# Where the gate weights are loaded and summed, and where the first blocks' tiles lie, in a two-layer graph network kernel

## The chip, the cores and the metric

The kernel runs on one core of a Trainium2 chip. A core has a matrix engine (TensorE, PE in the profile; its weight loads are shown apart as PEld), VectorE (DVE), ScalarE (ACT), GpSimd (POOL) and SyncE (SP), which here only issues transfers. Each engine works through its own instructions in order and waits on semaphores for the others. Transfers (DMAs) are issued by SP and by ScalarE, and 16 DMA engines carry them out.

The metric is the device time of one execution in microseconds, the median of three runs.

## The reference, cut to what matters

There are two layers over 128 graphs of 128 nodes with 256 features, all in float32. Only the first layer is touched by the change:

```python
h = jnp.maximum(_layernorm(x, axis=-1), 0.0)
# _L0_gnn_ref(h, ...):
xc = jnp.transpose(h, (0, 2, 1))
t = relu(bn(conv1d(xc, conv1_w, 0)))                 # 1x1 convolution
t = bn(conv1d(t, conv2_w, 8))                        # 17 taps along the nodes
x_conv = jnp.transpose(relu(t + xc), (0, 2, 1))
s = h @ w_se.T + b_se                                # 3 features
A = jnp.exp(-dist(s)) * adj
x_nmp = A @ relu(h @ w_msg.T + b_msg)
gi = concatenate([x_conv, x_nmp], -1) @ w_ih.T + b_ih
gh = h @ w_hh.T + b_hh                               # gates r, z, n from gi and gh
x = x + (1 - z) * n + z * h
```

The second layer applies five small graph convolutions to the first 25 nodes of each graph, with a softmax of `fusion_w` as their weights.

## The kernel before, in words

A block is 4 graphs (`BB`), so there are 32 blocks. A half is 64 graphs, 16 blocks. The 17-tap convolution is done in the frequency domain: 40 frequencies (`NP_`), for which the transformed inputs of one half are kept on chip in one tile `X` (80 KB per partition).

**Heads of the first half** (`heads` with h = 0). For each block: load x (`head_load`, tile `ln`), statistics (`head_stats`: VectorE, then one power on POOL, tile `rs`, L193), normalise (`head_norm`, VectorE, L199), transpose and relu (`head_turn`, L209 and L210), the first convolution (`head_conv1`, L223 to L227), the transform into `X` (`head_spectra`, L238 to L246). Between these steps the transform of the 17-tap weights runs (`weight_spectra`) and is written to DRAM as `vd`.

**Frequencies of the first half** (`spectral` with h = 0). Two frequencies at a time, 1 MB of `vd` is loaded by SP into a tile `v` (three buffers, two DMAs each, L291). For each frequency POOL adds two parts of `v` into `vs` (L306), VectorE combines two parts of `X` into `s` (L304), and TensorE runs two groups of matmuls, L309 on `vs` and L314 on `s` and `X`. ScalarE and VectorE bring the result into `ys` (L311, L315). After every four frequencies ScalarE issues two writes of `ys` to DRAM (`yd`). A table `amid` lets other work be issued ahead of a frequency: the first blocks of the second half are begun there (`heads_begin`), and so are the loads of `idm`, `wms`, `bms` and `fw` (`small_loads`, at frequency 8), of `wih` (at 12) and of `whh` (at 20).

**Heads of the second half** (`heads` with h = 1). The same as before, with three x blocks ahead. The function `between` that `heads` calls twice per block here steps the generator `gate_weights` (L333 to L337). It forms sums and differences of blocks of the gate weights on POOL, since `gates` multiplies 2 by 2 blocks with seven products instead of eight. There are twelve such adds of 128 x 384 elements, two per step.

**Frequencies of the second half** (`spectral` with h = 1, nothing amid).

**Blocks** (from L421). `load(i)` brings a block's inputs from DRAM: `ht` (three buffers), the adjacency `at`, and the frequency results `ym` and `yr` (two buffers each). For each block: `messages` (L505), `conv_out` (L487 on `ym`, L490 on `yr`), `edge_terms`, `edges`, `x_nmp` (L551), then `gates` (L599). The second layer's work runs between the gate products. `load(0)` and `load(1)` stand ahead of the first block, followed by the loads for the node degrees (`degree_loads`).

**What sets the order.** The first stage is issued in the order written. In the stages of the halves that holds for POOL throughout and for SP up to the end of the second half's heads (`manual_schedule`); elsewhere a scheduler may move an instruction ahead. The block phase's pool `wk` reuses the memory of the front stages. `reuse_waits="tile"` means that a new tile waits until the last use of each old tile that lay there. Tiles are laid out in the order in which `load` first asks for them. DMAs take eight completion semaphores in turn, so that a DMA waits for the landing of the eighth one before it.

Of the kernel before, what the change touches and what calls it, by code (L numbers as in the profile page):

```python
# [8 lines left out]
F32 = mybir.dt.float32  # L9
# [4 lines left out]
P = 128  # L14
# [3 lines left out]
BB = 4  # L18
# [3 lines left out]
NP_ = LW // 2  # L22
# [52 lines left out]
def gnn_kernel(ctx: ExitStack, tc: tile.TileContext, io, out0: bass.AP, out1: bass.AP):  # L75
    nc = tc.nc
    x, adjT = io["x"], io["adjT"]
    B, N, D = x.shape
    C = D // P
# [15 lines left out]
    def row(name, n):  # L95

        return bass.AP(tensor=io[name].tensor, offset=io[name].offset, ap=[[0, P], [1, n]])
# [16 lines left out]
    def constant_loads():  # L114
        nc.sync.dma_start(vec, io["vec"])
        nc.sync.dma_start(wc1, io["wc1"].rearrange("(c p) o -> p c o", p=P))
        nc.sync.dma_start(fd, io["fd"])
# [23 lines left out]
    fw = cst.tile([P, 5], F32)  # L141
# [35 lines left out]
    def head_load(pool, ahead, i, queue):  # L177
        xs[i] = pool.tile([P, BB, D], F32, tag="ln", name="ln", bufs=ahead)
        queue.dma_start(xs[i], x[i * BB:(i + 1) * BB].rearrange("b n d -> n b d"))

    def head_stats(wk, i, behind=None):

        mv = wk.tile([P, BB, 2], F32, tag="mv", name="mv", bufs=3)
        st = wk.tile([P, BB, 6], F32, tag="st", name="st", bufs=2)
        if behind is not None:
            nc.scalar.copy(st[:, :, 0], behind[:, :, 0])
        for b in range(BB):
            nc.vector.bn_stats(st[:, b, :], xs[i][:, b, :])
            nc.vector.bn_aggr(mv[:, b, :], st[:, b, :])
        ve = wk.tile([P, BB], F32, tag="ve", name="ve", bufs=2)  # L190
        nc.vector.tensor_scalar(ve, mv[:, :, 1], EPS, None, op0=ALU.add)  # L191
        rs = wk.tile([P, BB], F32, tag="rs", name="rs", bufs=3)
        nc.gpsimd.tensor_tensor(rs, ve, mhalf, op=ALU.pow)  # L193
        stats[i] = mv, rs
# [19 lines left out]
    def head_conv1(wk, i):  # L214
        ht = hcs.pop(i)
        h1 = wk.tile([P, BB, D], F32, tag="h1", name="h1", bufs=2)
        for h in range(BB // 2):
            ps = bank()
            pv = ps.rearrange("p (b d) -> p b d", b=2)
            for bb in range(2):  # L220
                b = 2 * h + bb
                for c in range(C):
                    nc.tensor.matmul(pv[:, bb, :], ht[:, c, b * N:(b + 1) * N], wc1[:, c, :],  # L223
                                     start=c == 0, stop=c == C - 1)
            hv = h1[:, 2 * h:2 * h + 2, :]
            nc.vector.tensor_tensor(hv, pv, sh1[:, None, :].to_broadcast([P, 2, D]), op=ALU.add)
            nc.scalar.activation(hv, hv, AF.Relu)  # L227
        h1s[i] = h1
# [32 lines left out]
    def heads(wk, xk, ahead, X, h, between):  # L261

        i0, i1 = h * NBH, (h + 1) * NBH
        for i in range(i0, i1 + 1):
            if i + ahead < i1:
                head_load(xk, ahead, i + ahead, nc.sync)
            if i < i1:
                head_conv1(wk, i)
            between()
            if i + 1 < i1:  # L270
                head_turn(wk, i + 1)
            if i + 2 < i1:
                head_norm(i + 2)
            between()
            if i > i0:
                head_spectra(X, i - 1)
            if h == 0 and i % 2:
                between()
            if i + 3 < i1:
                head_stats(wk, i + 3, h1s[i] if h else None)  # L280
# [59 lines left out]
    with front as es:  # L340
        hk = es.enter_context(tc.tile_pool(name="hk", bufs=1))
        xp = es.enter_context(tc.tile_pool(name="xp", bufs=1))
        X = xp.tile([P, C, NP_, 2, P], F32)
        order = es.enter_context(ExitStack())
        order.enter_context(tc.manual_schedule(engines={nc.gpsimd.engine}))
        sync_order = order.enter_context(ExitStack())
        sync_order.enter_context(tc.manual_schedule(engines={nc.sync.engine}))
        with ExitStack() as ws:

            ws.enter_context(tc.manual_schedule())  # L350

            xk = ws.enter_context(tc.tile_pool(name="xk", bufs=1, side="right"))
            wp = ws.enter_context(tc.tile_pool(name="wp", bufs=1))
            ahead = 5
            todo = [(c, q) for c in range(C) for q in range(D // WCH)]
            head_load(xk, ahead, 0, nc.scalar)
            nc.sync.dma_start(gt, io["gt"])
            taps = [taps_load(wp, *todo[0], nc.sync, split=4)]
            spectra = []

            def some_spectra(k=1):
                for _ in range(k):
                    if not spectra and todo:
                        spectra.append(weight_spectra(wp, *todo.pop(0), taps.pop(0)))
                    if spectra and next(spectra[0], STOP) is STOP:
                        spectra.pop(0)
                        if len(todo) > 1:
                            taps.append(taps_load(wp, *todo[1], nc.scalar))
                        some_spectra()

            constant_loads()
            head_load(xk, ahead, 1, nc.sync)
            taps.append(taps_load(wp, *todo[1], nc.sync))
            for k in range(2, ahead):
                head_load(xk, ahead, k, nc.sync)
            head_stats(hk, 0)
            some_spectra()
            head_norm(0)
            some_spectra()
            head_turn(hk, 0)  # L380
            constants()
            some_spectra()
            head_stats(hk, 1)
            some_spectra()
            head_norm(1)
            head_stats(hk, 2)
            some_spectra()
            heads(hk, xk, ahead, X, 0, some_spectra)
            while spectra or todo:
                some_spectra()  # L390
        gw = ctx.enter_context(tc.tile_pool(name="gw", bufs=1, side="right", reuse_waits="tile"))
        xk = es.enter_context(tc.tile_pool(name="xk1", bufs=1, reuse_waits="tile"))
        bp = es.enter_context(tc.tile_pool(name="bp", bufs=1, reuse_waits="tile"))
        idm = gw.tile([P, N], F32)
        wms = gw.tile([P, C, D + 3], F32)
        bms = gw.tile([P, D + 3], F32)
        wih = gw.tile([P, 2 * C, 3 * D], F32)
        whh = gw.tile([P, C, 3 * D], F32)
        sw = [gw.tile([P, 3, 3, P], F32, name=f"sw{k}") for k in range(3)]

        def small_loads():
            nc.sync.dma_start(idm, io["idm"])
            nc.sync.dma_start(wms, io["wms"].rearrange("(c p) o -> p c o", p=P))
            nc.sync.dma_start(bms, row("bms", D + 3))
            nc.sync.dma_start(fw, row("fw", 5))

        begin = heads_begin(hk, xk, 3, 1)
        sums = gate_weights()
        amid = {p: lambda: next(begin, None) for p in range(16, NP_, 4) if p != 20}
        amid[8] = small_loads  # L410
        amid[12] = lambda: nc.sync.dma_start(wih, io["wih"].rearrange("(c p) o -> p c o", p=P))
        amid[20] = lambda: nc.sync.dma_start(whh, io["whh"].rearrange("(c p) o -> p c o", p=P))
        spectral(bp, X, 0, amid)
        for _ in begin:
            pass
        heads(hk, xk, 3, X, 1, lambda: next(sums, None))
        sync_order.close()
        spectral(bp, X, 1, {})
        order.close()

    wk = ctx.enter_context(tc.tile_pool(name="wk", bufs=1, reuse_waits="tile"))  # L421
# [4 lines left out]

    def load(i):
        h, g0 = divmod(i * BB, HG)
        ht = wk.tile([P, C, T], F32, tag="ht", name="ht", bufs=3)
        nc.sync.dma_start(ht, htd[i])  # L430
        at = wk.tile([P, BB, N], F32, tag="at", name="at", bufs=2)
        nc.sync.dma_start(at, adjT[i * BB:(i + 1) * BB].rearrange("b m n -> m b n"))
        y = yd[h].rearrange("g w d o -> g (w d) o")[g0:g0 + BB]
        ym = wk.tile([P, BB, D], F32, tag="ym", name="ym", bufs=2)
        nc.sync.dma_start(ym, y[:, :P, :].rearrange("g r o -> r g o"))
        yr = wk.tile([P, D], F32, tag="yr", name="yr", bufs=2)
        for b in range(BB):
            nc.sync.dma_start(yr[b * NR:(b + 1) * NR, :], y[b, P:, :])
        loaded[i] = at, ym, yr
        hts[i] = ht  # L440
# [698 lines left out]
```

## Time and profile before

| what | value |
|---|---|
| median of 3 runs | 1935.14 us (1934.36 to 1942.66) |
| the profiled execution | 1944.77 us, span 1943.0 us |
| mean granted TensorE clock | 0.992 |
| instructions | 29921 |
| bytes moved by DMA | 265.76 MB, mean 137 GB/s |

The stages, from the timeline: the heads of the first half end near 175 us, its frequencies near 292, the heads of the second half near 402, its frequencies near 507, and the blocks fill the rest. The page's chain of work that ended last begins with this line:

```profile
PE 90%; DMA 6%; DVE 2%; issue 1%; ACT 1%; POOL 0%; SPq 0%; ACTq 0%; POOLq 0%; DVEq 0%
```

The chain is followed back from the last instruction, at each step to what released it. Nine tenths of it is TensorE itself. The rows of DMAs on the page that belong to the stages in question are these, with how often each is issued and how large one is:

```profile
v<-vd SPq DMA_DIRECT2D x80, 512.0 KB
yd<-ys ACTq DMA_DIRECT2D x40, 512.0 KB
```

So each half's frequencies read 20 MB of `vd` and write 10 MB of `yd`.

### The profile page before, as it was taken

How to read it: one execution, taken by the hardware profiler on the slowest of the kernel's cores; microseconds unless marked ns; L12 is line 12 of the kernel's file. 1: busy time of each engine (PE TensorE's matmuls, PEld its weight loads, DVE VectorE, ACT ScalarE, POOL GpSimd, SP SyncE). 2: the span in 40 equal slices, each digit the busy share in tenths (PEclk: the TensorE clock that was granted, in tenths of full speed). 3: DMA queues.
4: the chain of work that ended last, by engine and by line, in shares of the span. 5: the costliest groups of instructions: out<-in, count | busy, mean ns of one | idle time of the engine just before them, and what ended most of it. 6: DMA issues, size and time to landing. Idle time of an engine off the chain costs nothing.

```text
span 1943.0 us, 29921 instructions
## 1 busy us (share of the span) xinstructions
PE 1901.1 (98%) x10418; PEld 1652.7 (85%) x10418; DVE 1296.3 (67%) x3247; ACT 713.2 (37%) x1459; POOL 609.2 (31%) x681
## 2 busy tenths in 40 slices
PE   8999898999899999999999999999999999999999
PEld 7888787988788888888888888888878888888887
DVE  5676457754587777777756577787756587777643
ACT  4553113421143334334333434334334434333334
POOL 1012442135233433443322243343322143343300
PEclk9999999999899999999999999999999999999999
DMA  8787975459843223233323533224333523222125
GB/s 309 293 315 226 323 260 194 142 181 309 267 135 98 72 72 102 68 81 110 81 84 92 142 81 100 70 71 116 86 82 87 147 75 105 74 72 64 44 88 154
DMA packets 248853, 265.76 MB, mean 137 GB/s; under 512 B 106850, under 2 KB 223927, under 8 KB 244223
## 3 DMA queue, kind: packets, MB, share of 16 engines
q1 hardware_dynamic: 236767, 196.74, 35.8%
q10 hardware_dynamic: 11936, 67.11, 8.9%
q8 instruction: 83, 1.36, 0.3%
q14 instruction: 67, 0.55, 0.1%
HBM read 178.66 MB, written 85.14 MB: 136 GB/s over the span
## 4 chain that ended last, share of the span: by engine, by line
PE 90%; DMA 6%; DVE 2%; issue 1%; ACT 1%; POOL 0%; SPq 0%; ACTq 0%; POOLq 0%; DVEq 0%
PE bank L599 44%; PE bank L314 6%; PE bank L505 5%; PE bank L919 5%; PE bank L859 5%; PE bank L223 5%; PE bank L487 3%; PE bank L551 3%; PE bank L238 3%; DMA v<-vd 3%; PE bank L309 3%; PE bank L490 1%; PE bank L162 1%; PE bank L538 1%; PE bank L838 1%; PE bank L770 1%
## 5 line engine op out<-in xcount | busy, mean ns | idle before, releaser
L599 PE MATMUL bank<-t,sw 128*128 128x256 f32 x1152 | 290.9, 379 | 0.2 <-POOL t L573 0.2
L612 POOL TENSOR_TENSOR u<-u,m 128x256 f32<-128x256 f32 x128 | 92.9, 726 | 594.4 <-ACT m L610 532.2
L599 PEld LDWEIGHTS bank<-t,sw 128*128 128x128 f32 x1152 | 215.3, 190 | 30.1 <-issue 2.3
L599 PE MATMUL bank<-t,wih 128*128 128x256 f32 x768 | 197.2, 379 | 0.0
L599 PEld LDWEIGHTS bank<-t,wih 128*128 128x128 f32 x768 | 143.4, 190 | 19.3 <-DVE u L617 0.5
L306 POOL TENSOR_TENSOR vs<-v 128x512 f32<-128x512 f32 x78 | 100.5, 1307 | 138.7 <-DMA v<-vd 74.9
L223 PE MATMUL bank<-wc,ht 128*128 128x256 f32 x512 | 125.1, 399 | 6.1 <-ACT ht L210 6.1
L505 PE MATMUL bank<-wms,ht 128*128 128x259 f32 x512 | 122.3, 381 | 0.0
L223 PEld LDWEIGHTS bank<-wc,ht 128*128 128x128 f32 x512 | 100.4, 201 | 22.6 <-ACT ht L210 8.4
L599 PE MATMUL bank<-t,whh 128*128 128x256 f32 x384 | 114.6, 380 | 0.3 <-DVE z L614 0.3
L599 PE MATMUL bank<-xc,wih 128*128 128x256 f32 x384 | 114.7, 380 | 0.0
L599 PE MATMUL bank<-xn,wih 128*128 128x256 f32 x384 | 114.6, 380 | 0.0
L919 PE MATMUL bank<-w,hh 128*125 128x256 f32 (+9 forms) x480 | 113.5, 380 | 0.3 <-DVE hh L864 0.3
L599 PE MATMUL bank<-ht,whh 128*128 128x256 f32 x384 | 110.3, 381 | 0.0
L505 PEld LDWEIGHTS bank<-wms,ht 128*128 128x128 f32 x512 | 97.3, 190 | 14.7
L304 DVE SCALAR_TENSOR_TENSOR s<-X 128x256 f32<-128x256 f32 x78 | 48.0, 618 | 90.4 <-PE bank L314 90.1
L859 PE MATMUL bank<-ax,w 128*128 128x500 f32 (+8 forms) x416 | 107.0, 396 | 0.0
L617 DVE TENSOR_TENSOR u<-bank,u 128x256 f32<-128x256 f32 x128 | 53.7, 420 | 74.0 <-PE bank L599 74.0
L919 PEld LDWEIGHTS bank<-w,hh 128*125 128x125 f32 (+9 forms) x480 | 84.3, 177 | 18.6 <-issue 0.9
L509 ACT ACTIVATE msg<-msg 128x512 f32<-128x512 f32 x64 | 40.3, 630 | 162.0 <-DVE msg L506 160.2
L193 POOL TENSOR_TENSOR rs<-ve,mhalf 128x4 f32<-128x4 f32 x32 | 32.3, 1010 | 211.7 <-DVE ve L191 211.7
L311 ACT COPY k<-bank 128x256 f32<-128x256 f32 x78 | 29.0, 373 | 179.4 <-PE bank L309 70.2
(191 smaller groups left out, 4305.3 us busy)
## 6 DMA issues: line engine op xcount, KB each, us to landing
v<-vd SPq DMA_DIRECT2D x80, 512.0 KB
vd<-sp ACTq DMA_DIRECT2D x8, 2560.0 KB
yd<-ys ACTq DMA_DIRECT2D x40, 512.0 KB
w<-in_w_dram SPq DMA_DIRECT2D x40, 512.0 KB
htd<-ht ACTq DMA_DIRECT2D x32, 512.0 KB
ht<-htd SPq DMA_DIRECT2D x32, 512.0 KB
ym<-yd SPq DMA_DIRECT2D x32, 512.0 KB
xt<-in_xT_dram SPq DMA_DIRECT2D x32, 512.0 KB
```

The source lines that it names most:

```text
L223: nc.tensor.matmul(pv[:, bb, :], ht[:, c, b * N:(b + 1) * N], wc1[:, c, :], start=c == 0, stop=c == C - 1)
L238: nc.tensor.matmul(ps[:, bb * 2 * LW:(bb + 1) * 2 * LW], h1[:, 2 * h + bb, c * P:(c + 1) * P], fd, start=True, stop=True)
L306: nc.gpsimd.tensor_tensor(vs, vr, vi, op=ALU.add)
L309: nc.tensor.matmul(p1[:, :D], a[:, c], vs[:, c], start=c == 0, stop=c == C - 1)
L314: nc.tensor.matmul(ps[:, k * D:(k + 1) * D], u[:, c], w[:, c], start=c == 0, stop=c == C - 1)
L487: nc.tensor.matmul(ps[:, b * N:(b + 1) * N], ym[:, b, o * P:(o + 1) * P], idm, start=b == 0, stop=False)
L505: nc.tensor.matmul(ps[:, :D + 3], ht[:, c, b * N:(b + 1) * N], wms[:, c, :], start=c == 0, stop=c == C - 1)
L551: nc.tensor.matmul(ps[:, b * N:(b + 1) * N], msg[:, b, c * P:(c + 1) * P], e[:, b, :], start=True, stop=True)
L599: nc.tensor.matmul(ps, w, d, start=n == 0, stop=n == len(pairs) - 1)
L612: nc.gpsimd.tensor_tensor(got["u4"], got["u2"], got["m5"], op=ALU.add)
L859: nc.tensor.matmul(pv[:, q - q0, :], w1s[k5 + g][:, c, q * P:(q + 1) * P], xv[:, c], start=c == 0, stop=c == C - 1)
L919: nc.tensor.matmul(ps[:n1, :D], hh[:, q, at:at + n1], w2s[k5 + g][:, q, :], start=q == 0, stop=q == HID // P - 1)
```

## The change

It has three parts.

- The load of `fw` (five numbers, for the second layer's softmax) moves from `small_loads` to the start, behind the first five x blocks. The few VectorE and ScalarE instructions that use it are moved by the scheduler from around the second half's frequencies to the first heads.
- The other weight loads move from the first half's frequencies to the heads of the second half. A new generator `gate_loads` takes the place of `gate_weights` as what `heads` steps between its parts; `wih` is loaded in two DMAs. The sums of `gate_weights` move to the frequencies of the second half, one step ahead of every fourth frequency from 4 on.
- `load` asks for its tiles in another order: `at`, `yr` and `ym` come before `ht`. With that `yr` of block 0 no longer lies on `X`, and `ht` of block 1 does. The order of the DMAs stays.

The order of TensorE's instructions is the same in both programs. POOL's adds L333 to L337 stand among L306 instead of L193.

```diff
             for k in range(2, ahead):
                 head_load(xk, ahead, k, nc.sync)
+            nc.sync.dma_start(fw, row("fw", 5))
...
             nc.sync.dma_start(bms, row("bms", D + 3))
-            nc.sync.dma_start(fw, row("fw", 5))
...
         amid = {p: lambda: next(begin, None) for p in range(16, NP_, 4) if p != 20}
-        amid[8] = small_loads
-        amid[12] = lambda: nc.sync.dma_start(wih, io["wih"].rearrange("(c p) o -> p c o", p=P))
-        amid[20] = lambda: nc.sync.dma_start(whh, io["whh"].rearrange("(c p) o -> p c o", p=P))
         spectral(bp, X, 0, amid)
         for _ in begin:
             pass
-        heads(hk, xk, 3, X, 1, lambda: next(sums, None))
+
+        def gate_loads():
+            yield
+            small_loads()
+            yield
+            yield
+            nc.sync.dma_start(wih[:, :C], io["wih"][:D].rearrange("(c p) o -> p c o", p=P))
+            yield
+            yield
+            nc.sync.dma_start(wih[:, C:], io["wih"][D:].rearrange("(c p) o -> p c o", p=P))
+            yield
+            yield
+            nc.sync.dma_start(whh, io["whh"].rearrange("(c p) o -> p c o", p=P))
+
+        loads = gate_loads()
+        heads(hk, xk, 3, X, 1, lambda: next(loads, None))
         sync_order.close()
-        spectral(bp, X, 1, {})
+        spectral(bp, X, 1, {p: lambda: next(sums, None) for p in range(4, NP_, 4)})
+        for _ in sums:
+            pass
...
     def load(i):
         h, g0 = divmod(i * BB, HG)
+        at = wk.tile([P, BB, N], F32, tag="at", name="at", bufs=2)
+        yr = wk.tile([P, D], F32, tag="yr", name="yr", bufs=2)
+        ym = wk.tile([P, BB, D], F32, tag="ym", name="ym", bufs=2)
         ht = wk.tile([P, C, T], F32, tag="ht", name="ht", bufs=3)
         nc.sync.dma_start(ht, htd[i])
-        at = wk.tile([P, BB, N], F32, tag="at", name="at", bufs=2)
         nc.sync.dma_start(at, adjT[i * BB:(i + 1) * BB].rearrange("b m n -> m b n"))
         y = yd[h].rearrange("g w d o -> g (w d) o")[g0:g0 + BB]
-        ym = wk.tile([P, BB, D], F32, tag="ym", name="ym", bufs=2)
         nc.sync.dma_start(ym, y[:, :P, :].rearrange("g r o -> r g o"))
-        yr = wk.tile([P, D], F32, tag="yr", name="yr", bufs=2)
```

## The prediction

> **What bounds the kernel now.** I read, in this order: the busy shares on the page, the list of what TensorE waited for, the busy table cut at the stages that the diff touches, and the timeline around each TensorE gap. TensorE is busy for nearly the whole span, so time can come only from its gaps and from its clock.
>
> ```profile
> PE 1901.1 (98%) x10418; PEld 1652.7 (85%) x10418; DVE 1296.3 (67%) x3247; ACT 713.2 (37%) x1459; POOL 609.2 (31%) x681
> PEclk9999999999899999999999999999999999999999
> ```
>
> 1943.0 - 1901.1 leaves 41.9 us of gaps. The mean granted clock of 0.992 costs another 1943 x 0.008 = 15 us. The list of waits says who ended the gaps:
>
> ```profile
> PE bank L162 <- DMA w<-in_w2t_dram: 7.8, 2, 5.7
> PE bank L223 <- ACT ht L210: 6.1, 6, 2.9
> PE bank L309 <- POOL vs L306: 5.9, 4, 3.0
> PE bank L314 <- issue: 4.5, 2, 2.5
> PE bank L490 <- DMA yr<-yd: 2.9, 1, 2.9
> ```
>
> Rows two to five lie in four stages: the frequencies of the first half, the heads of the second half, the frequencies of the second half, and the start of the block phase. Their busy table:
>
> ```profile
> 175.10:291.80 116.70, 106.26 (x482) 91.33 (x482) 54.95 (x98) 16.16 (x43) 53.20 (x43) 0.99 0.84 278
> 291.80:402.00 110.20, 104.68 (x620) 94.89 (x619) 82.89 (x260) 47.77 (x135) 24.84 (x24) 0.98 0.45 157
> 402.00:507.00 105.00, 105.00 (x494) 92.55 (x493) 49.71 (x83) 16.05 (x45) 47.13 (x39) 1.00 0.83 274
> 507.00:526.00 19.00, 14.07 (x61) 11.13 (x60) 9.67 (x22) 4.15 (x7) 6.08 (x8) 0.76 0.89 250
> ```
>
> The columns are length, then busy PE, PEld, DVE, ACT, POOL, then clock, DMA share, GB/s. The two halves do the same frequency work. The second half, without weight loads among its `v` loads, has no gap at all. The first half has 10.4 us of gaps. The places, from the timeline:
>
> ```profile
> 191.94 0.77 SPq L411 DMA_DIRECT2D wih<-in_wih_dram  x1
> 237.07 1.78 DVE L199 TENSOR_SCALAR ln<-ln,mv,rs 128x256 f32<-128x256 f32 x2 [5.14 <-POOL rs L193]
> 240.35 2.03 PE L314 MATMUL bank<-v,s 128*128 128x256 f32 x4 [1.99 <-issue]
> 301.26 4.31 DVE L199 TENSOR_SCALAR ln<-ln,mv,rs 128x256 f32<-128x256 f32 x4 [1.13 <-POOL rs L193]
> 307.37 0.70 PE L223 MATMUL bank<-wc,ht 128*128 128x256 f32 x2 [2.93 <-ACT ht L210]
> 330.77 1.38 DVE L199 TENSOR_SCALAR ln<-ln,mv,rs 128x256 f32<-128x256 f32 x4 [1.12 <-POOL rs L193]
> 507.12 1.98 SPq L438 DMA_DIRECT2D yr<-yd  x4
> 514.37 1.19 PE L490 MATMUL bank<-idr,yr 128*128 128x256 f32 x2 [2.94 <-DMA yr<-yd]
> 515.00:520.00 5.00, 5.00 (x16) 3.31 (x14) 2.17 (x3) 1.61 (x3) 0.72 (x1) 0.50 0.95 284
> ```
>
> The same four L199 take 4.31 us at 301 and 1.38 at 331: at 301 four gate sums run on POOL beside them, at 331 none do. The five microseconds after the `yr` gap run at clock 0.50.
>
> [...] after 2.98 us of idle at 194.8 no slow slice shows, so not every gap pays. [...]
>
> **The change part by part.** The instruction lists of both programs show the same order on TensorE. So each part is only a matter of what comes late.
>
> *Loads out of the first half's frequencies.* Removed there: idm, wms, bms, fw (455 KB), wih 1536 KB, whh 768 KB, together 2.8 MB, or 10 us at that stage's 278 GB/s. The gaps are 2.98 + 1.73 + 0.92 + 0.29 = 5.9 us before L309 (`v` late, hence `vs` late) and 1.99 + 2.53 = 4.5 us before L314. The latter come from VectorE: L199 stands in front of `s` (L304) and waits for `rs`, which sits on POOL behind the `vs` of a late tile. The slice 240 to 245 has clock 0.66, another 1.7 us. All of it: 12.1. The 5.9 should go, as in the second half. The order L199 before `s` stays: with the second half's timing `vs` of frequency 23 would end as TensorE starts L309 of 22, and rs 1.0 + two L199 0.75 + s 0.42 = 2.2 us set against the 0.86 us of that L309 still stalls about 1.4. For the three norms I keep 2 us. Gain 10 (5 to 12).
>
> *The same loads among the second half's heads.* DMA share is 0.45 there, 157 GB/s. 2.8 MB add 26 GB/s over 110 us. Each lies in SP's queue between x loads that are 6.5 us apart; 768 KB need 2.8 us. Only the first three meet the last `v` tiles, near 297 to 304, where the queue is full; the x block loaded then is read about 6 us later. Cost 0 (0 to 3).
>
> *Sums out of these heads.* Both L199 groups shrink from 4.31 to 1.38 us. The first sum burst ends in gaps of 2.93 and 0.31, the second in 0.93 and 0.31; ScalarE then offers `ht` at about 304.5 against TensorE's 304.4, so some 0.4 stays. The slices 305 to 315 have clocks 0.86 and 0.79: 0.7 + 1.05 = 1.75 us. Gain 4.1 + 1.4 = 5.5 (3 to 6.5). The fill gap of 1.06 at 297.6 stays.
>
> *Sums into the second half's frequencies.* Twelve adds of 1.0 us, in pairs of 2.15 before frequencies 4 to 24. POOL goes from 47 to 60 of 105 us. POOL idles between the `vs` of one tile and of the next: the six places have 1.46 us or more. At frequency 12 the idle is 1.60, so `vs` comes 0.55 later, and it now leads L309 by 434.36 - 431.83 = 2.5. At 20 the lead is only 0.26, but the idle before it is 3.63. [...] This cover is all that hides 12.9 us. Cost 0.5 (0 to 12).
>
> *Tiles laid out elsewhere.* In the program's layout `yr` of block 0 lay on the tile X, so its four loads waited at SP for the last L314 at 506.7, with everything of block 1 behind them. Now at, yr and ym of block 0 lie below X and block 1's `ht` reaches into it instead. The `yr` loads go out near 498 to 500 behind 1.4 MB (ht, at, ym, idr; about 5 us at 274 GB/s), landing by 505; L490 wants them at 511.4. Block 1's ht then waits for X in their place, issued near 507 instead of 512.3, and is read at 526.7. Gain 2.94, plus 1.6 of the 2.5 us that the 0.50 slice costs; the 1.99 us gap before L551, VectorE's `e`, remains [...]. Gain 4.5 (2.9 to 5.5).
>
> *fw load early.* Its six tiny VectorE instructions (about 0.16 us each, as L191 shows) and one ScalarE exponential move into the first heads. Between x loads it should land near 19 us (4.9 MB at about 330 GB/s); VectorE reads it at 23.5. Two come just ahead of the add L226 at 33.2. Cost 0.5 (0 to 1.5, more if fw lands late, because VectorE's whole queue waits behind the reduction).
>
> Sum: 10 + 5.5 + 4.5 - 0 - 0.5 - 0.5 = 19 us. The profiled execution took 1944.77, 9.6 above the median of 1935.14. The trace does not say where those 9.6 went. The 57 us of gaps and slow clock are the natural place, and the change removes a third of that, so I take a third of 9.6, about 3, as already absent from the median run: 1935 - 16 = 1919.
>
> **Rivals.**
> 1. The first half stays bound by its own `v` and `yd` traffic (DMA share 0.84) and by L199 before `s`; only 3 of the 10 come. For: after the weight loads were through, gaps still came at 231, 238 and 263. Against: the second half has the same traffic and none. Gain 12, less the 3: 1926.
> 2. The loads make the x blocks late among the heads, undoing that 5.5 and costing 2: gain about 11, less 2: 1926. Against: share 0.45.
> 3. The other side. The pairs of sums hold up `vs` in the second half. It begins to cost once pair 2.15 exceeds idle plus lead, 4.1 at frequency 12. Then TensorE stops up to 2.15 us six times (12.9), each stop followed by a slow slice of 1.7 (10), and `s` blocked for 0.9 us on a dozen frequencies (11). 34 us against 20 gained: 1947.
> 4. Everything goes, the norm stalls and the whole 0.50 slice too: 24 us, 1911 or less.
>
> **How the numbers follow.** Forecast 0.58 at 1919, own range 1911 to 1926; rival 1 0.17, rival 2 0.08, rival 3 0.09, rival 4 0.08. A difference of 0.5%, 9.7 us, is about what a measurement of this kernel tells from none: faster means below 1925.5. Faster: 0.54 of the forecast + 0.08 + 0.05 + 0.03 = 0.70; slower 0.09; the rest 0.21. The range 1909 to 1932 leaves out rival 3 and the far ends.
>
> **What would show it.** Right: the first half's frequencies take about 106 us from first L309 to last L314, with no wait on POOL `vs`; four L199 take about 1.4 us at every head; no wait of L490 on `yr`, no 0.50 slice; the second half still without gaps. Wrong: waits of L309 on `vs` in the second half, x loads landing after VectorE is ready, VectorE waiting for fw near 24 us, or the first half's gaps unchanged.

## The result, and the profile after

| | before | after |
|---|---|---|
| median, runs side by side | 1939.41 us (14 runs, 1932.32 to 1944.15) | 1929.74 us (14 runs, 1922.02 to 1935.02) |
| profiled execution | 1944.77 us, span 1943.0 | 1930.41 us, span 1928.7 |

The ratio is 0.995, with a 95% interval from 0.9936 to 0.9964: a gain of 9.7 us, between 7.0 and 12.4. The forecast was 19 us on the profiled execution and 16 on the median. The measured time lies above the forecast's own range of 1911 to 1926 us, though within the outer one of 1909 to 1932. Part of that is the base, whose median over 14 runs is 4.3 us higher than over the three runs of the prediction. The gain itself is 9.7 of the 16 us forecast for the median; the two profiled executions differ by 14.4, against 19.

The busy shares and the clock on the page of the changed kernel:

```profile
PE 1900.0 (99%) x10418; PEld 1654.8 (86%) x10418; DVE 1288.2 (67%) x3247; ACT 712.2 (37%) x1459; POOL 610.3 (32%) x681
PEclk9899999999999999999999999999999999999999
```

TensorE's gaps are 1928.7 - 1900.0 = 28.7 us instead of 41.9. Who ended them is in its list of waits (us in total, times, longest):

```profile
PE bank L162 <- DMA w<-in_w2t_dram: 7.7, 2, 5.8
PE bank L565 <- DVE e L555: 2.4, 2, 2.1
...
PE bank L309 <- POOL vs L306: 2.4, 1, 2.4
PE bank L723 <- DVE dinv L718: 2.3, 1, 2.3
...
PE bank L223 <- ACT ht L210: 1.6, 3, 1.1
...
PE bank L314 <- DVE s L304: 0.2, 1, 0.2
PE bank L314 <- issue: 0.2, 1, 0.2
```

Lines from L434 of the kernel before are 14 higher here: L490 is L504, L551 is L565, L709 is L723. The wait on `yr` is gone, L223 and L309 wait a good deal less. One line is larger than before, L723 on `dinv`, which had 0.8 us. It will matter.

The busy table at the same four stages (length, then busy PE, PEld, DVE, ACT, POOL, then clock, DMA share, GB/s):

```profile
178.40:285.80 107.40, 104.64 (x485) 90.60 (x484) 53.04 (x92) 15.99 (x42) 49.25 (x39) 1.00 0.84 273
285.80:392.70 106.90, 105.06 (x635) 95.79 (x634) 79.01 (x266) 48.60 (x139) 18.89 (x18) 1.00 0.55 191
392.70:495.20 102.50, 102.50 (x476) 90.06 (x475) 48.80 (x79) 15.00 (x40) 58.19 (x49) 1.00 0.85 282
495.20:507.80 12.60, 10.42 (x56) 8.60 (x56) 6.58 (x18) 4.04 (x7) 6.09 (x8) 0.91 0.83 222
```

As these lines stand, they seem to confirm the sum term by term: the first half's frequencies from 117 to 107 us, the second half's heads from 112 to 107, the second half's frequencies without a gap although 58 us of POOL lie there, the start of the blocks from 17.5 to 12.6. That is 20 us. (The values of before are taken between the marks below, which put the heads at 112.3 us; the prediction's table cuts them at rounder times.) A pair of profiles is not the median, however, and two stages lie outside this table: the first heads, and the first two blocks. The experiments had to tell where 20 us became 10.

**How stages are measured below.** From the traces, between marks that exist in every variant: the first heads end with the first L309, a half's frequencies end with the last L314 of that half, the second half's heads lie between, the start of the blocks ends with the first gate product (L599 before, L613 after), and "two blocks" are the gates of blocks 0 and 1 with all between them. Blocks 2 to 31 took 1292.43 or 1292.44 us in all seventeen traces, so nothing is to be found there. Half clock means a spell in which the trace records a granted TensorE clock of 0.50; what is lost to it is estimated as half the length of the spell (in the run with late transposes and the old layout sixteen L238 took 4.63 us in such a spell and 2.44 outside).

### The profile page after: what moved, and what is told of

The parts are those of the page before. It is cut to its first block, busy times and chain, and to the rows that moved or that the text cites. A ratio compares the mean times of both kernels' runs of the same rounds, so it can differ in the third digit from the quotient of the medians.

```text
span 1928.7 us, 29906 instructions
## 1 busy us (share of the span) xinstructions
PE 1900.0 (99%) x10418; PEld 1654.8 (86%) x10418; DVE 1288.2 (67%) x3247; ACT 712.2 (37%) x1459; POOL 610.3 (32%) x681
## 4 chain that ended last, share of the span: by engine, by line
PE 88%; DMA 5%; DVE 4%; POOL 1%; issue 1%; ACT 1%; SPq 0%; ACTq 0%; POOLq 0%; DVEq 0%
PE bank L613 43%; PE bank L314 6%; PE bank L519 5%; PE bank L933 5%; PE bank L873 5%; PE bank L223 4%; PE bank L309 3%; PE bank L565 3%; PE bank L501 3%; PE bank L238 3%; PE bank L162 2%; PE bank L552 1%; PE bank L504 1%; DMA v<-vd 1%; PE bank L852 1%; PE bank L784 1%
## 5 line engine op out<-in xcount | busy, mean ns | idle before, releaser
L613 PE MATMUL bank<-t,sw 128*128 128x256 f32 x1152 | 291.1, 380 | 0.0
L613 PEld LDWEIGHTS bank<-t,sw 128*128 128x128 f32 x1152 | 215.7, 190 | 29.7 <-issue 2.3
L613 PE MATMUL bank<-t,wih 128*128 128x256 f32 x768 | 197.2, 379 | 0.0
L613 PEld LDWEIGHTS bank<-t,wih 128*128 128x128 f32 x768 | 143.4, 190 | 19.3 <-issue 0.5
L306 POOL TENSOR_TENSOR vs<-v 128x512 f32<-128x512 f32 x78 | 101.4, 1320 | 115.8 <-DMA v<-vd 54.1
L223 PE MATMUL bank<-wc,ht 128*128 128x256 f32 x512 | 121.0, 389 | 1.7 <-ACT ht L210 1.6
L613 PE MATMUL bank<-t,whh 128*128 128x256 f32 x384 | 114.9, 381 | 0.0
L613 PE MATMUL bank<-xc,wih 128*128 128x256 f32 x384 | 114.7, 380 | 0.0
L613 PE MATMUL bank<-xn,wih 128*128 128x256 f32 x384 | 114.3, 379 | 0.1
L223 PEld LDWEIGHTS bank<-wc,ht 128*128 128x128 f32 x512 | 97.8, 196 | 16.6 <-ACT ht L210 3.6
L613 PE MATMUL bank<-ht,whh 128*128 128x256 f32 x384 | 110.3, 381 | 0.0
L873 PE MATMUL bank<-ax,w 128*128 128x500 f32 (+8 forms) x416 | 107.0, 396 | 0.3 <-DMA w<-in_w_dram 0.3
L193 POOL TENSOR_TENSOR rs<-ve,mhalf 128x4 f32<-128x4 f32 x32 | 32.3, 1008 | 222.3 <-DVE ve L191 222.3
L304 DVE SCALAR_TENSOR_TENSOR s<-X 128x256 f32<-128x256 f32 x78 | 49.0, 631 | 80.0 <-PE bank L314 79.8
L653 ACT ACTIVATE nn<-nn,vec 128x512 f32<-128x512 f32 x64 | 46.2, 722 | 129.6 <-DVE nn L652 129.6
```

Of the source, the lines that this page charges most:

```text
L306: nc.gpsimd.tensor_tensor(vs, vr, vi, op=ALU.add)
L613: nc.tensor.matmul(ps, w, d, start=n == 0, stop=n == len(pairs) - 1)
L873: nc.tensor.matmul(pv[:, q - q0, :], w1s[k5 + g][:, c, q * P:(q + 1) * P], xv[:, c], start=c == 0, stop=c == C - 1)
```

## The experiments
Each part was done alone, or left out alone. All variants compute the whole result, and every one left a trace, so a stage that a variant doesn't touch is one more draw of that stage.

**The layout alone**: `load` asks for `at`, `yr`, `ym` ahead of `ht`, the rest as before.

```diff
+        at = wk.tile([P, BB, N], F32, tag="at", name="at", bufs=2)
+        yr = wk.tile([P, D], F32, tag="yr", name="yr", bufs=2)
+        ym = wk.tile([P, BB, D], F32, tag="ym", name="ym", bufs=2)
         ht = wk.tile([P, C, T], F32, tag="ht", name="ht", bufs=3)
...
```

> The kernel before with only the block phase's tiles laid out as in the changed kernel. Theory A (each part does what its stage shows: the start of the block phase 17.5 to 12.6 us, and nothing elsewhere): no wait on yr, start of the blocks about 12.6 us, rest as before, median about 4.9 us under the kernel before (ratio 0.9975). Rival B (the layout gives it back later: the first two blocks +1.3 and the tail +1.1 us, as in the profile of the changed kernel): the start as in A, first two blocks 79.3 instead of 78.0 and tail 44.8 instead of 43.7, median 2.5 us under before (0.9987).

1938.16 us against 1940.23, ratio 0.9988 (0.9973 to 1.0003). Start 13.1 us, two blocks 79.9. The ratio's interval still holds theory A's 0.9975, so it doesn't decide; the trace has the longer two blocks of rival B: the gain is given back.

**The early `fw` alone.**

```diff
+            nc.sync.dma_start(fw, row("fw", 5))
             head_stats(hk, 0)
...
-            nc.sync.dma_start(fw, row("fw", 5))
```

> The kernel before with only the fw load moved to the start. Theory A: nothing, the first heads' stage 175 us give or take the half-clock spells that fall in it, no wait of VectorE on fw, ratio 1.000 within 0.001. Rival C (the early fw load and its six VectorE instructions cost what the first heads lost in the changed kernel): first heads' stage 178.4 us, new TensorE gaps behind VectorE near 24 to 70 us, median 3 us over before (1.0017).

Ratio 0.9993 (0.998 to 1.0005), first heads 174.3 us. Rival C falls. What stands out is a stage that this variant doesn't touch: the first half's frequencies took 110.4 us, not 117.

**The weight loads and the sums moved, without layout and early `fw`**, and **the changed kernel without the early `fw`** (the same, with the layout).

```diff
...
+        loads = gate_loads()
+        heads(hk, xk, 3, X, 1, lambda: next(loads, None))
         sync_order.close()
...
+        spectral(bp, X, 1, {p: lambda: next(sums, None) for p in range(4, NP_, 4)})
```

> The changed kernel without the layout and without the early fw: only the weight loads and the sums are moved. Theory A: first half's frequencies about 107 us instead of 117, second half's heads about 107 instead of 112, yr still waits near 511 (start of the blocks 17.5 us), first heads 175; median 15 us under before (0.992). Rival D (executions other than the profiled one hold fewer late v tiles before, so that the loads' place is worth less on the median): the same stage times in the profile, but a median of only 6 to 8 us under before (0.996 to 0.997).

> The changed kernel with fw loaded with the other small loads, not at the start. Theory A: as the changed kernel, 1930 us, 9.7 us under before (0.995); the half-clock spells in the first heads fall differently again. Rival C (early fw costs 3 us in the first heads): first heads 175 us, 13 us under before (0.9933).

The first: 1928.68 us, ratio 0.9945 (0.9927 to 0.9963). The second: 1929.25, ratio 0.9947 (0.9927 to 0.9966). So the two moves carry the whole gain, and the layout adds nothing measurable to them. Theory A's 15 us are outside the interval of the first; of rival D's 6 to 8 us only the upper end is inside. The gain lies between the two. First half's frequencies 109.6 and 107.9 us.

In both, the second half's heads took 108.2 and 108.7 us, against 106.9 in the changed kernel. VectorE's timeline of the second run, which has the layout but not the early `fw`, shows what is different (start, duration, engine, line, then in brackets the idle time ahead and what ended it):

```profile
281.41 0.16 DVE L466 TENSOR_REDUCE fmx<-fw 128x1 f32<-128x5 f32 x1 [6.25 <-DMA fw<-in_fw_dram]
281.61 0.23 DVE L468 TENSOR_SCALAR fsb<-fw,fmx 128x5 f32<-128x5 f32 x1
281.75 1.88 DVE L315 TENSOR_TENSOR ys<-bank,k 128x512 f32<-128x512 f32 x3
```

With `fw` loaded among the heads, VectorE's queue stands 6.25 us (6.63 in the first run) on twenty bytes per partition, at the end of the first half's frequencies, and three `ys` that were due come in one burst. The early load is what removes this wait. The 1.3 to 1.8 us that follow are not all shown to come from it: TensorE's own waits among the heads are 3.0 and 2.2 us against 1.6, and the second run also loses 1.7 us there to half clock.

**The sums alone**, the loads left in the first half:

```diff
-        heads(hk, xk, 3, X, 1, lambda: next(sums, None))
+        heads(hk, xk, 3, X, 1, lambda: None)
...
+        spectral(bp, X, 1, {p: lambda: next(sums, None) for p in range(4, NP_, 4)})
```

> The kernel before with only the sums moved into the second half's frequencies; the weight loads stay in the first half's. Theory A (the loads are free among the heads): second half's heads 106.5 to 107.5 us, as with the loads there too (106.9 to 108.7), second half's frequencies 102.5 to 103.9. Rival E (the loads among the heads cost about 1 us of the 5.5): 105.5 to 106.5 us. First half's frequencies, with the loads still there, 110 to 117 us as in the three executions with loads so far (117.1, 111.9, 110.4); if they come out under 109 the loads are not what sets them. Median 4 us under before (0.998).

1933.34 us, ratio 0.997 (0.9959 to 0.9982). Second half's heads 106.6 us, the same as with the loads there and `fw` early; so rival E falls, and no cost of 2.8 MB more among the heads shows. First half's frequencies 110.3. The median is 5.5 us under before; with the loads moved as well it was 11.6 under, so the loads' place is worth about 6 us by the medians.

**The kernel before, profiled again.**

> The kernel before, unchanged, profiled a second time. Theory F (the first profiled execution drew a long first half of frequencies, 117.1 us, where 110.4 and 111.9 are usual with the same code): 110 to 113 us with 5 to 7 us of gaps, all stages from the second half's heads on within 0.2 us of the first profile save for half-clock spells. Rival G (117 is usual for the kernel before, and the two variants had shorter ones by chance): 115 to 118 us with about 10 us of gaps.

First half's frequencies 114.1 us, with 6.5 us of gaps and 3.4 us lost to half clock. That is above theory F's 113 and below rival G's 115. The gaps fit F. Its TensorE timeline there:

```profile
210.32 1.16 PE L309 MATMUL bank<-vs,X 128*128 128x256 f32 x4 [3.06 <-POOL vs L306]
235.57 2.08 PE L309 MATMUL bank<-vs,X 128*128 128x256 f32 x4 [2.57 <-POOL vs L306]
264.94 1.10 PE L314 MATMUL bank<-v,s 128*128 128x256 f32 x4 [0.86 <-issue]
```

The waits on a late `v` are there again, 33 and 58 us into the stage, near two of the places they had before (35 and 57); the one at 23 is gone. The waits of L314 are 0.86 us, not 4.5.

**The large loads from POOL's queue**, at the same frequencies and with the same bytes:

```diff
-        amid[12] = lambda: nc.sync.dma_start(wih, io["wih"].rearrange("(c p) o -> p c o", p=P))
-        amid[20] = lambda: nc.sync.dma_start(whh, io["whh"].rearrange("(c p) o -> p c o", p=P))
+        amid[12] = lambda: nc.gpsimd.dma_start(wih, io["wih"].rearrange("(c p) o -> p c o", p=P))
+        amid[20] = lambda: nc.gpsimd.dma_start(whh, io["whh"].rearrange("(c p) o -> p c o", p=P))
```

> The kernel before with wih and whh issued from POOL's queue at the same frequencies of the first half, so that no v load stands behind them in SP's queue; the bytes are the same. If v is late because of the order in one queue: waits of L309 on vs under 1.5 us in sum and the first half's frequencies 107 to 109 us, as with the loads moved away (106.7 to 109.6). If it is the bytes: waits of L309 3.5 to 6 us and 110 to 114 us, as in the five executions with the loads (110.3 to 117.1). In either case L314 keeps its wait of 1 to 3 us, which was the same with the loads (0.9 to 4.5) and without (0.4 to 3.2).

```profile
194.10 1.13 PE L309 MATMUL bank<-vs,X 128*128 128x256 f32 x4 [1.62 <-POOL vs L306]
210.68 1.13 PE L309 MATMUL bank<-vs,X 128*128 128x256 f32 x4 [0.77 <-POOL vs L306]
235.22 1.10 PE L314 MATMUL bank<-v,s 128*128 128x256 f32 x4 [2.22 <-issue]
251.71 1.13 PE L309 MATMUL bank<-vs,X 128*128 128x256 f32 x4 [1.57 <-POOL vs L306]
```

This is TensorE's timeline: waits on `vs` of 1.62 + 0.77 + 1.57 = 3.96 us, and 111.4 us for the stage. In sum that is where the five with the loads on SP are (3.75 to 5.92 us of such waits), and outside the eleven without (0 to 2.35). But POOL's timeline has the first large load behind the first of these waits:

```profile
197.93 0.93 POOL L411 DMA_DIRECT2D wih<-in_wih_dram  x1
```

So the 1.62 us at 194.1 can't come from it. A wait at this place, some 22 us into the stage, stands in three of the five with the loads and in four of the eleven without. The waits behind that place make 2.34 us, inside what the five have there (1.4 to 5.6) and also at the upper end of the eleven (0 to 2.35). POOL, which makes `vs`, also spends 0.93 and 0.72 us on issuing the two loads. One execution of this kind doesn't tell whether the bytes or the place in SP's queue make `v` late.

**What the layout's gain turns into.** Block 1's `ht` and, behind it in SP's queue, `dga` (which VectorE's reduction for the degrees reads, L680 before and L694 after) are the next to look at. SP's timeline, first of the kernel before, then of the changed one:

```profile
507.12 1.98 SPq L438 DMA_DIRECT2D yr<-yd  x4
512.32 0.34 SPq L430 DMA_DIRECT2D ht<-htd  x1
...
516.46 0.42 SPq L665 DMA_DIRECT2D dga<-in_adjF_dram  x1
```

```profile
491.88 2.96 SPq L452 DMA_DIRECT2D yr<-yd  x4
500.40 0.34 SPq L447 DMA_DIRECT2D ht<-htd  x1
...
505.48 0.42 SPq L679 DMA_DIRECT2D dga<-in_adjF_dram  x1
```

The last L314 ends at 507.0 and at 495.2. `yr` goes out 3.3 us ahead of that end instead of 0.1 behind it. But `ht` of block 1 goes out 5.3 us behind it in one and 5.2 in the other, and `dga` 9.4 and 10.3. The release of X is not what holds this `ht`: the list of SP's waits in the kernel before puts 3.2 us on a write of `yd`. By the semaphores that the traces record, in both kernels, it is the first of the last two `yd` writes of the second half, which used the completion semaphore that this `ht` takes. That write landed at 512.30 in one and at 500.33 in the other, and `ht` went out at 512.32 and 500.40. (For the changed kernel the list of waits names an L539 of TensorE instead, whose signal came at 500.38, when the wait was already over.) VectorE's timeline of the changed kernel shows who pays:

```profile
503.86 0.90 DVE L555 TENSOR_TENSOR e<-e,at 128x512 f32<-128x512 f32 x1 [1.27 <-ACT e L554]
510.31 1.53 DVE L694 TENSOR_REDUCE dinv<-dga 128x53 f32<-128x1325 f32 x1 [5.55 <-DMA dga<-in_adjF_dram]
511.76 0.68 DVE L568 COPY xn<-bank 128x512 f32<-128x512 f32 x1
```

VectorE stands 5.55 us for `dga` (0.66 before), with `xn` and the whole chain to `dinv` behind it. Two attempts to bring `dga` earlier, from POOL's queue and then, with `nc.sync` in the same place, from SP's:

```diff
-        a = l1.tile([P, FL, NN], F32, tag="f", name="dga", bufs=1)
-        nc.sync.dma_start(a, io["adjF"])
...
+    dga = l1.tile([P, FL, NN], F32, tag="f", name="dga", bufs=1)
+    nc.gpsimd.dma_start(dga, io["adjF"])
     load(0)
     load(1)
-    degs = degrees(*degree_loads())
+    degs = degrees(dga, *degree_loads())
```

> The changed kernel with one load, dga (VectorE's reduction for the degrees reads it), taken out of SP's queue and issued from POOL's, where it need not stand behind block 1's loads. Theory A (the layout's gain is given back because block 1's ht still waits for the last store of the second half, as before, and dga with it, so that VectorE stands about 5.5 us for dga in front of xn): dga issued near 498 and landed by 503 to 505 instead of 510.3, VectorE's wait for it under 1.5 us, no wait of L613 or L723 over 1 us, first two blocks 76 to 77.5 us instead of 79.3, median about 3 us under the changed kernel. Rival B (the two blocks are longer because of half-clock spells alone): dga lands earlier, but the blocks stay at 79 to 81 us.

> As the run with dga from POOL, but dga stays in SP's queue and only passes four to six of block 1's loads. Theory A: dga issued near 501.5 instead of 505.5, VectorE's wait for it some 4 us shorter than the 5.55 of the changed kernel, first two blocks 77 to 78 us. Rival B: 79 to 81 us.

The first: 1926.94 us, ratio 0.9935 (0.9918 to 0.9953), two blocks 77.0; the second, one execution, 76.9. The rival of these two runs, that the two blocks are longer because of half clock alone, falls, though half clock has a part: they lose 1.0 and 0.6 us to it here against 2.2 in the changed kernel. Yet the start took 16.1 and 19.4 us, which theory A had not foreseen. In VectorE's timeline of the second:

```profile
502.71 1.53 DVE L692 TENSOR_REDUCE dinv<-dga 128x53 f32<-128x1325 f32 x1 [6.29 <-DMA dga<-in_adjF_dram]
504.16 0.68 DVE L555 TENSOR_TENSOR e<-e,at 128x512 f32<-128x512 f32 x1
```

With `dga` asked for earlier, the scheduler put its reduction ahead of `e`, on which TensorE waits. Start and two blocks together took 93.2 and 96.4 us, against 91.9 in the changed kernel: the wait only changed its place. So the next runs leave the load and move what waits for it.

**The reductions behind block 0's `xn`, and `dinv`'s transposes (L723) four steps later**; then **the transposes alone**. The first adds a copy of one column (`after`, a part of `xn`'s sums) that the reduction then overwrites; the second has the new `range` only.

```diff
+        nc.vector.tensor_copy(dinv[:, F0:F0 + 1], after)
         nc.vector.reduce_sum(dinv[:, F0:K0], a, axis=AX.X)
...
-        for _ in range(3):
+        for _ in range(7):
             yield
```

> The changed kernel with the degrees' reductions tied behind block 0's xn on VectorE and their transposes (L723) put four steps later on TensorE, so that nothing stands behind dga. Theory A (the layout's gain at the start of the blocks is given back through dga): the stretch from the last L314 to the end of the second block, 91.9 us in the changed kernel, 92.4 to 95.5 without the layout, falls to 88 to 89.5, no wait of L723 or L613 over 0.7 us, median 3 us under the changed kernel, about 1926.5. Rival H (block 1's ht, late by the same store, is read by TensorE too and stalls it next): the stretch stays at 91 to 93 with a new wait of L519 on ht.

> The changed kernel with only the transposes of dinv put four steps later on TensorE; the reductions stay where they are. Theory A: no wait of L723 (2.3 us in the changed kernel), but VectorE still stands some 5.5 us for dga in front of xn, so L613 may wait up to 2.4 us: the stretch from the last L314 to the end of the second block 89.5 to 91 us. If it stays at 92, L723's wait was not what was given back.

The first missed: 1928.38 us, ratio 0.9936 (0.9918 to 0.9955), start and two blocks 92.5 us. That is rival H's number, but not its wait on `ht`: TensorE waited 2.87 us for `rt` and 1.08 for `lr`. Its VectorE now stood for the next load in the row, with block 1's messages behind it:

```profile
512.76 1.72 DVE L703 TENSOR_REDUCE dinv<-dgb 128x60 f32<-128x1500 f32 x1 [4.25 <-DMA dgb<-in_adjK_dram]
514.39 0.14 DVE L694 COPY dinv<-t 128x1 f32<-128x1 f32 x1
514.45 0.42 DVE L520 TENSOR_TENSOR msg<-bank,bms 128x256 f32<-128x256 f32 x1
```

The second hit, in one execution: 89.9 us, no wait of L723. **The same, timed, and both without the layout:**

> The kernel of e8_turn_late again (dinv's transposes four steps later on TensorE, nothing else), now timed. Theory A (with the layout the block phase starts 4 us earlier while dga comes no earlier, and TensorE pays for it at L723): stretch from the last L314 to the end of the second block about 90 us again, no wait of L723, median 2 us under the changed kernel's, near 1927 to 1928 (ratio to before 0.994). If e8_turn_late's 89.9 was a lucky draw: 91.5 to 93 us and the median of the changed kernel, 1929 to 1930.

> The same later transposes, but the tiles laid out as before. Theory A: the yr wait stands, and L723 had only 0.8 to 1.7 us to lose here, so the stretch is 91.5 to 93 us and the median 2 to 3 us over the run with the layout. Rival I (the layout is worth nothing even when nothing is late behind it): stretch and median within 1 us of the run with the layout.

> The run with the degrees tied behind xn, without the new layout. Theory A: yr waits again (2.9 us and a half-clock spell), the stretch from the last L314 to the end of the second block 91.5 to 93 us, that is 3.5 to 4.5 more than with the layout; median 4 us over that run. Rival I (the layout is worth nothing even then): within 1 us of that run.

Transposes late, with the layout: 1927.55 us, ratio 0.9932 (0.9911 to 0.9953), start and two blocks 90.2. Without: 1928.17, 0.9938 (0.9916 to 0.996), 91.3. With the reductions also tied, without the layout: 1928.04, 0.995 (0.9937 to 0.9963), 95.3, against 92.5 with it. Theory A had 2 to 3 us for the first pair and gets 1.1 in the trace, where neither of the two loses anything to half clock, and 0.6 in the medians. That is nearer to rival I; the intervals are too wide to part them. The 2.8 us of the second pair are not the layout's: there the run without it loses 3.4 us more to half clock, and the medians, 1928.38 with and 1928.04 without, show no gain. TensorE's timeline of the first shows what is still late:

```profile
508.28 0.70 PE L613 MATMUL bank<-xn,wih 128*128 128x256 f32 x2 [1.95 <-DVE xn L568]
```

That is `xn`, behind the reduction that stands for `dga`. None of the variants is shown to beat the changed kernel; their intervals and its own overlap.

**The changed kernel, profiled again.**

> The changed kernel, unchanged, profiled a second time. If 10 us was too much for the first half's frequencies because the one profile of before drew a long one: 106.5 to 109 us here. Second half's heads 106.5 to 107, stretch from the last L314 to the end of the second block 91.5 to 93 us with a wait of L723 of 1 to 2.5 us, and the first heads 172 to 178 us, the width that the other executions showed with fw early or late.

First half's frequencies 106.5 us, second half's heads 107.0, start and two blocks 92.2, first heads 174.4, all within what was expected. Not so the wait of L723, 0.77 us instead of 1 to 2.5: most of the loss stands at `xn` this time. Both places of the give-back show in TensorE's timeline:

```profile
508.36 0.70 PE L613 MATMUL bank<-xn,wih 128*128 128x256 f32 x2 [2.18 <-DVE xn L568]
...
524.33 0.42 PE L723 MATMUL bank<-ident,dinv 128*53 128x128 f32 x2 [0.77 <-DVE dinv L718]
```

## Why the prediction was wrong, by its own steps

The stages of all seventeen traces, grouped by what matters to the stage (mean, lowest to highest, number of executions):

| stage | as before | as changed | predicted gain | measured |
|---|---|---|---|---|
| first half's frequencies | 112.8 (110.3 to 117.1), 5 | 107.4 (106.1 to 109.6), 11 | 10 | 5.4 |
| second half's heads | 112.1 (111.7 to 112.3), 5 | 106.7 (106.6 to 107.0), 9 with `fw` early | 5.5 | 5.4 |
| second half's frequencies | 102.7 (102.5 to 103.6), 5 | 103.5 (102.6 to 105.5), 12 | -0.5 | -0.8 |
| start of the blocks | 16.1 (15.6 to 17.5), 6 | 12.2 (11.5 to 13.1), 4 | 4.5 | 3.9 |
| two blocks | 77.0 (76.3 to 78.0), 6 | 80.3 (79.3 to 81.2), 4 | 0 | -3.3 |
| first heads | 175.0 (172.8 to 177.2), 7 | 175.3 (171.8 to 181.2), 10 | -0.5 | 0 within its scatter |

5.4 + 5.4 - 0.8 + 3.9 - 3.3 = 10.6 us, and the medians say 9.7. The two rows on the blocks count only kernels whose degrees are as before; the first row leaves out the run with the loads on POOL's queue.

**The step that failed first: "Loads out of the first half's frequencies", gain 10 (5 to 12).** It was the sum of one execution's gaps. By who ended the gap:

| mean of the executions | profile of before | with the loads (5) | without (11) |
|---|---|---|---|
| L309 on `vs`, `v` late | 5.9 | 4.9 | 0.9 |
| L314 (read as `s` behind L199) | 4.5 | 1.9 | 2.0 |
| lost to half clock | 1.7 | 1.4 | 0 |

The first row's reading was right in kind: late `v` tiles, and most of this wait goes with the loads. Waits some 34 and 56 us into the stage stand in all five with the loads; of the eleven without, one has a wait near the first of these places and none near the second. Its size was too high by 2 us: the 5.9 was the highest of the five, and 0.9 stays. The second was wrong. The prediction kept 2 us for the norms and charged the other 2.5 to the loads; over the executions this wait is the same with and without them, and 4.5 was the highest of sixteen. The 5 at the lower end of the range had the right size; the 10 took one draw for the rule. That the second half has no gap was no evidence for 4.5: it has no norms among its frequencies either. That the loads' place ahead of `v` in SP's queue makes it late was the author's reading, and it isn't shown: at a DMA share of 0.84 the bytes alone are a rival, and the run with the loads on POOL's queue, 2.34 us of waits behind the first of them, doesn't part the two.

**The second: "Tiles laid out elsewhere", gain 4.5.** The gap on `yr` went, as said, and the start is 3.9 us shorter: 2.7 us of waits and 1.3 of half clock, in the means. The sentence that failed is "Block 1's ht then waits for X in their place, issued near 507 instead of 512.3". It had priced the queue up to X and not what holds `ht` beyond it. Nothing of block 1 and of the degrees comes earlier with respect to the end of the frequencies, so TensorE, now 4 us ahead, meets `xn` and `dinv` late: its waits for these two in the two blocks grow from 1.0 to 2.8 us, and all its waits there from 1.8 to 3.4. That is half of the 3.3 us. The other half is half clock, of which 1.9 us fall in these two blocks with the layout and 0.3 without, while in the start it falls from 2.0 to 0.7. So the forecast's 1.6 us for the 0.50 slice didn't come either. Over the start and the two blocks together the four executions with the layout lose 1.7 to 3.4 us to half clock, the six without 1.7 to 5.1, and the means are 2.6 and 2.3.

The net 0.6 agrees with the layout alone (0.9988) and with the pair that differs only in it (0.9945 and 0.9947 with `fw` late). Shown: which waits and how much half clock make up the 3.3 us, that VectorE stands for `dga` there, and that moving L723 back removes its wait. Not shown: why the half clock moved, and that the layout is worth its full 4 us once nothing is late behind it, since the one variant that freed `xn` as well made VectorE stand for `dgb` instead.

**What held.** The sums out of the heads: L199 took 4.31 us beside POOL's sums and takes 1.38 in the changed kernel's VectorE timeline, as in the lines below, and most of the gaps ahead of L223 go with it. Taken one by one in the kernel before, an L199 lasted 1083 to 1155 ns in the group at 301, with the sums on POOL, and 406 to 412 ns in the group at 331, with nothing there. It isn't "at every head", though: the last of the thirteen groups takes 4.91 us beside three `vs` and a sum on POOL (4.24 beside `vs` in the kernel before), and a gap of 0.27 us of TensorE follows.

```profile
305.42 1.38 DVE L199 TENSOR_SCALAR ln<-ln,mv,rs 128x256 f32<-128x256 f32 x4 [1.12 <-POOL rs L193]
311.69 1.38 DVE L199 TENSOR_SCALAR ln<-ln,mv,rs 128x256 f32<-128x256 f32 x4 [1.12 <-POOL rs L193]
```

The sums into the second half's frequencies cost 0.8 us on the mean and 2.8 at most, so rival 3's 34 us never came near, though the sign that it named shows: L309 waits 0.7 to 2.4 us on `vs` in six of the twelve executions with the sums there, and 0.77 in one of the five without. That a slow slice follows every stop was the author's estimate and isn't shown. Of its blocked `s` little shows: in this stage of the changed kernel `s` (L304) took 407 to 1337 ns, median 468, against 409 to 1504, median 426, in the kernel before. (Two of its sums are off: 1935 - 20 + 34 is 1949 and not 1947, and rival 4's 1911 leaves out the 3 us that the forecast takes off.) No cost of the loads among the heads shows. Rival 1 was nearest for the first stage: 2.0 us of the wait at L314 and 0.9 of late `v` stay, though 5 us went and not 3.

**`fw`.** No price in the first heads shows above their scatter, and the prediction missed the early load's use. In the kernel before, the instructions on `fw` ran at 187 to 194 us, in the first half's frequencies and not around the second half's, as the part on the change has it. With the loads moved and `fw` left among them, they hold up VectorE where the second half's heads begin, and the second half's heads take 108.4 us instead of 106.7, in part through half clock. It asked what the early load costs, not what a late one would.

**The base.** The prediction took a third of 9.6 us as absent from the median of three runs. Over 14 runs that median is 1939.41, so the profiled execution was 5.4 above it and the three runs 4.3 below. The extra was mostly in the first half's frequencies: 117.1 against a mean of 112.8.

## What to carry to other kernels

Before the gaps of a stage are added up as a gain, ask which of them would fall in the same place in a second execution; at a DMA share of 0.84 the single profile here held waits of 4.5 us at one line that were 1.9 in the mean. When a wait at a queue's head is removed, follow the next instructions of that queue to what each is released by: what isn't released earlier stays where it was (here `ht` of block 1, 5.3 us behind the end of the frequencies before and 5.2 after), and the engine that was sped up meets it a few microseconds on. A small load that a reduction waits for should be issued well ahead of it, because the engine's whole queue waits with it: VectorE's stood 6.25 us on `fw` loaded among the heads, and not at all on `fw` loaded at the start of the changed kernel. As `dga` shows, on which VectorE then stood 6.29 us ahead of `e`, it must also be seen that the reduction doesn't move ahead with its load.

## What the runs showed of the hardware

TensorE's half clock isn't repeatable. The first 175 us are the same code in all executions but for `fw`, and lost 3.4 to 11.9 us to half clock, which alone makes up most of that stage's scatter (171.8 to 181.2 us). Two lines of the run with late transposes and the old layout, from the busy table (length, PE and so on, clock after POOL's column), show that TensorE's gaps don't tell when it comes:

```profile
85.90:92.70 6.80, 6.80 (x64) 6.32 (x60) 2.44 (x8) 2.62 (x9) 0.00 (x0) 0.50 0.52 161
504.00:510.80 6.80, 4.72 (x29) 3.53 (x30) 3.00 (x4) 2.48 (x5) 3.26 (x4) 1.00 0.98 314
```

The first slice has no gap at all, and the last one ahead of it is 0.21 us at 83.4; it runs at half clock. The second begins just after a gap of 2.96 us on `yr`; it runs at full clock, where seven other executions with a gap of 2.8 to 3.5 us on `yr` lost 1.5 to 3.8 us in the start of the blocks. So a slow spell can't be charged to one gap with confidence. What does repeat is its length: in the profiled executions of before and after, every spell but the one at the end lasted 3.41, 6.83 or 10.24 us.

A single load took 7.4 us from its issue on POOL's queue to its landing (`dga`, 0.68 MB, issued 1 us behind the last writes of `yd` and just ahead of block 1's loads), so being asked for early was not yet being there early.
